# A shared expert's last result added in rows by fours, and expert weights asked for matrix by matrix

## The chip, the cores and the metric

One core of a Trainium2 chip runs the whole kernel. The metric is the device time of one execution in microseconds (us), the median of several runs. Engines are named as the profile names them: PE is TensorE's matmul, PEld its weight load, DVE is VectorE, ACT is ScalarE, POOL is GpSimd, SP is SyncE; a q behind a name is the engine's queue of instructions that issue DMAs or wait.

## The reference: what is computed

Inputs are x (4 sequences of 512 tokens, 512 features, float32) and a context (4 x 1601 x 512). The first half is a cross-attention with 16 heads over two groups of keys (1344 and 257), each with its own softmax, and a residual. The second half is a mixture of experts with a residual:

```
x  = x + cross_attention(layernorm(x), ctx)
h  = layernorm(x)                              # 2048 tokens x 512
idx, w = router(h)                             # 4 of 32 experts per token
for e in range(32):                            # at most 80 tokens each
    Y = (silu(X_e @ W_gate[e]) * (X_e @ W_up[e])) @ W_down[e]
    out[tokens of e] += Y * w
shared = (silu(h @ shared_gate.T) * (h @ shared_up.T)) @ shared_down.T
return x + out + shared
```

X_e are the tokens that chose expert e. W_gate[e] and W_up[e] are 512 x 256, W_down[e] is 256 x 512, all float32; the shared expert has 512 inner features.

## The kernel before, in words

A hand-written order of work (no scheduler) is recorded in Python, engine by engine. The attention of the four batches comes first. Then a stage of shared-expert units for batches 0 to 2 runs beside the routing, and from about 1477 us on the 32 experts follow one another.

**The shared expert.** `shared()` makes small units, each one matmul group of four matmuls: for each batch n, four `gate` and four `up` units that fill `hT` (512 inner features in four chunks of 128 partitions, by 512 tokens), then four `down` units, each with 128 tokens. For batches 0 to 2 (`n < BEFORE`, BEFORE is 3) `down` adds the residual row `x1r` and writes `out`. For the last batch, whose residual is already in `out`, `down` copies each 128 x 512 result into one chunk of the tile `ys` (L973), and the fourth one issues a single accumulating DMA from POOL that adds `ys` into the 512 rows of `out` (L976). In `ys` a partition p holds the tokens p, 128+p, 256+p and 384+p, so each of the 512 pieces is one row of 512 floats, 2 KB.

**The experts.** Turn e of the main loop records, in this order: `gate_up(e)` (32 matmuls of 80 columns), the gather of the tokens of e+7, `turn(e+2)` (transposes of gathered tokens), `down(e-1)` (two matmul groups of 512 columns, ACT's scaling into `y` at L1029, and POOL's indirect accumulating DMA that scatters the 80 rows of `y` into `out`, L1030), then the weights of expert e+4, and at certain turns one shared unit of the last batch, from the list `between` (12 units: eight gate and up, four down).

**What orders the DMAs.** Each scatter, and the shared accumulation, adds into `out`, so each waits on POOL's queue until the one ahead of it has landed. Gathers stand on the same queue between the scatters. Weights go over SP's queue, which holds nothing else in this stage. `expert_weights(e)` asks for `W_gate`, `W_up` and `W_down` of one expert (512 KB each, L908) into pools of five buffers each; a request waits on SP's queue until the matmuls that read its buffer are done. Called after `down(e-1)` for e+4, it takes the buffers of expert e-1. PSUM is a ring of eight banks.

The lines that place the shared units of the last batch (L1103):

```
while done < n_between and done * (E - 4) < n_between * (e + 1):
    between.pop(0)()
    done += 1
```

Of the kernel before, what the change touches and what calls it, by code (L numbers as in the profile page):

```python
# [9 lines left out]
F32 = mybir.dt.float32  # L10
BF16 = mybir.dt.bfloat16
I32 = mybir.dt.int32
AF = mybir.ActivationFunctionType
ALU = mybir.AluOpType
# [4 lines left out]
P = 128  # L19
B, L, D = 4, 512, 512  # L20
# [4 lines left out]
NC = D // P  # L25
NG4 = 4
NQ = L // P
T = B * L
NT = T // P
E, I, TOPK, NG, TKG = 32, 256, 4, 8, 3  # L30
EG = E // NG
CAP = 80
NI = I // P
# [25 lines left out]
@with_exitstack  # L59
def xattn_moe_kernel(ctx: ExitStack, tc: tile.TileContext, a: dict, out: bass.AP):  # L60
    nc = tc.nc

    dram = ctx.enter_context(tc.tile_pool(name="dram", bufs=1, space=DRAM))
    x1_d = dram.tile([T, D], F32, name="x1_d")

    xw_d = dram.tile([T, D + E], F32, name="xw_d")
    xnT_d = dram.tile([P, NC, T], F32, name="xnT_d")
    den_d = dram.tile([B * NC, 2 * NG4, L], F32, name="den_d")
    rec_d = dram.tile([B * NC, 2 * NG4, L], F32, name="rec_d")

    const = ctx.enter_context(tc.tile_pool(name="const", bufs=1))
    ident = const.tile([P, P], F32, name="ident")
    make_identity(nc, ident)
    mhalf = const.tile([P, 8], F32, name="mhalf")
    nc.gpsimd.memset(mhalf, -0.5)
    logits = const.tile([P, NT, E], F32, name="logits")

    with tc.manual_schedule():
        body(tc, a, ident, mhalf, logits, x1_d, xw_d, xnT_d, den_d, rec_d, out)


BEFORE = 3
# [27 lines left out]
def body(ctx, tc, a, ident, mhalf, logits, x1_d, xw_d, xnT_d, den_d, rec_d, out):  # L110

    nc = tc.nc
    early = ctx.enter_context(ExitStack())

    def pool(name, bufs, to=ctx, **kw):
        return to.enter_context(tc.tile_pool(name=name, bufs=bufs, **kw))
# [8 lines left out]
    def psum(dt=F32):  # L125

        shape = [P, 512] if dt is F32 else [P, NQ, P]
        banks.append(banks.pop(0))
        return ring.tile(shape, dt, name="ps", tag=f"bank{banks[-1]}")
# [8 lines left out]
    def wide(name, keep=False):  # L138

        n = wides.pop(0)  # L140
        t = pt.tile([P, NC, 512], F32, name=name, tag=f"wide{n}")
        if keep:
            return t, n
        wides.append(n)
        return t
# [4 lines left out]
    def held(name):  # L150
        return hold.tile([P, D], F32, name=name, tag="hold")
# [27 lines left out]
    _, n, s0, _ = BLOCKS[0]  # L179
# [42 lines left out]
    def project(ps, lhsT, rhs):  # L222

        for c in range(NC):
            nc.tensor.matmul(ps, lhsT=lhsT(c), rhs=rhs(c), start=c == 0, stop=c == NC - 1)
# [447 lines left out]
    for n in range(2):  # L673
        t = w.tile([P, NQ, P], BF16, name=f"parts{n}", tag=f"parts{n}")
# [6 lines left out]
    for b in range(B):  # L681
# [14 lines left out]
        ws = (wv, wvi)  # L696
# [73 lines left out]
        for bl in range(NB):  # L770
            for c in range(NC):
# [7 lines left out]
                n = 7 if bl < 2 else 0  # L779
# [16 lines left out]
        for c in range(NC):  # L796
# [7 lines left out]
            fill, done = [], 0  # L804
# [22 lines left out]
            for t in range(NKT):  # L827
# [8 lines left out]
                if t == 1:  # L836
                    if more:
# [3 lines left out]
                        done = 1  # L841
# [59 lines left out]
    aoT_last = aoT  # L901


    def expert_weights(e):
        ws = []
        for name, shape in (("W_gate", [P, NC, I]), ("W_up", [P, NC, I]), ("W_down", [P, NI, D])):
            t = wgp.tile(shape, F32, name=name, tag=name)
            nc.sync.dma_start(t, a[name][e])  # L908
            ws.append(t)
        return ws  # L910

    SHARE = 2.4
    AHEAD, WEIGHTS = 7, 5

    def tokens():

        past = ew.tile([E, CAP], F32, name="past", bufs=1)
        nc.vector.tensor_scalar(past, best, T + 0.5, float(T), ALU.is_gt, ALU.mult)
        nc.vector.scalar_tensor_tensor(past, past, float(T), best, ALU.add, ALU.subtract)
        ps = psum()  # L920
        nc.tensor.transpose(ps[:CAP, :E], past, ident[:E, :E])
        nc.vector.tensor_copy(tok, ps[:CAP, :E])

    def shared():


        units = [[], []]
        downs = []
        xTs = {0: first_xT[0]}

        def fetch_x(n):
            xTs[n] = wide("xT")
            nc.sync.dma_start(xTs[n], xnT_d[:, :, n * L:(n + 1) * L])

        for n in range(B):
            t = {}

            def gate(ic, n=n, t=t):
                if ic == 0:
                    t["hT"] = wide("hT")  # L940
                if ic == 2 and n + 1 < B:
                    fetch_x(n + 1)
                ps = psum()
                project(ps, lambda k: sg[:, k, ic * P:(ic + 1) * P], lambda k: xTs[n][:, k, :])
                nc.scalar.activation(t["hT"][:, ic, :], ps, AF.Silu)

            def up(ic, n=n, t=t):
                ps = psum()
                project(ps, lambda k: su[:, k, ic * P:(ic + 1) * P], lambda k: xTs[n][:, k, :])
                nc.vector.tensor_tensor(t["hT"][:, ic, :], t["hT"][:, ic, :], ps, ALU.mult)  # L950
                if n == 0 and ic == NC - 1:
                    wides.append(first_xT[1])

            def fetch(j, n=n, t=t):
                t[j] = held("x1r")
                nc.sync.dma_start(t[j], x1_d[n * L + j * P:n * L + (j + 1) * P, :])

            def down(j, n=n, t=t, fetch=fetch):
                rows = slice(n * L + j * P, n * L + (j + 1) * P)
                if n < BEFORE:  # L960
                    if j == 0:
                        fetch(0)
                    if j + 1 < NQ:
                        fetch(j + 1)
                ps = psum()
                project(ps, lambda k: t["hT"][:, k, j * P:(j + 1) * P], lambda k: sd[:, k, :])
                if n < BEFORE:
                    nc.vector.tensor_tensor(t[j], t[j], ps, ALU.add)
                    nc.sync.dma_start(out[rows, :], t[j])
                    return  # L970
                if j == 0:
                    t["ys"] = wide("ys")
                nc.scalar.copy(t["ys"][:, j, :], ps)  # L973
                if j == NQ - 1:
                    to = out[n * L:(n + 1) * L, :].rearrange("(j p) d -> p j d", p=P)
                    nc.gpsimd.dma_start(to, t["ys"], accum_op=ALU.add)  # L976

            to = units[n >= BEFORE]
            if n == BEFORE:
                units[0] += downs  # L980
                downs = []
            for ic in range(NC):
                to += [partial(gate, ic), partial(up, ic)]
                if ic < 2:
                    to += downs[2 * ic:2 * ic + 2]
            downs = [partial(down, j) for j in range(NQ)]
        units[1] += downs
        return units

    def expert_parts():  # L990
# [49 lines left out]
        return weights, gather, turn, gate_up, down  # L1040

    units, between = shared()
    wo = weight("o_w", wide("wo"))
    for u in units[:2]:
# [5 lines left out]
    wgp = pool("wgp", WEIGHTS, side="right", reuse_waits="tile")  # L1050
# [3 lines left out]
    weights, gather, turn, gate_up, down = expert_parts()  # L1054
# [9 lines left out]
    for i, u in enumerate(units):  # L1064
        if i < 2:
            continue
        if i == len(units) - 2:
            for f in first + second:
                f()
            first, second = [], []  # L1070
            tokens()
            for e in range(AHEAD):
                gather(e)
        u()
        for f in side.get(i, ()):
            f()
        later.step()
        if i == ready:

            space = mid.tile([P, 2, L], F32, name="rb")  # L1080
            second = sum(routing(B - 1, space.rearrange("p k t -> p (k t)")), [])

        while spent < (i - 1) * SHARE and (first or i > ready and second):
            todo = first or second
            spent += 0.8 if len(todo) < 2 * CAP // 8 else 0.3
            todo.pop(0)()
        if i % 4 == 0 and i // 4 - 1 < WEIGHTS:
            weights[i // 4 - 1] = expert_weights(i // 4 - 1)
    turn(0)
    turn(1)  # L1090
    n_between, done = len(between), 0
    for e in range(E + 1):
        if e < E:
            gate_up(e)
            if e + AHEAD < E:
                gather(e + AHEAD)
        if e + 2 < E:
            turn(e + 2)
        if e:
            down(e - 1)  # L1100
            if e + WEIGHTS - 1 < E:
                weights[e + WEIGHTS - 1] = expert_weights(e + WEIGHTS - 1)
        while done < n_between and done * (E - 4) < n_between * (e + 1):  # L1103
            between.pop(0)()
            done += 1

# [36 lines left out]
```

## Time and profile before

| what | value |
|---|---|
| median of 3 runs | 1721.97 us (1720.85 to 1722.82) |
| the profiled execution's own time | 1721.27 us |
| its span | 1719.6 us |
| granted TensorE clock, mean | 0.994 |
| PE busy | 1680.5 us (98%) |
| DVE, ACT, POOL busy | 981.4 us (57%), 651.1 us (38%), 864.5 us (50%) |
| W_gate, W_up, W_down requests | 32 of each, 512 KB a piece |
| the shared accumulation `out<-ys` | one, 1024 KB, issued at 1668.2 us |
| scatters `out<-y,tok` | 32, from 1493.2 to 1712.0 us |

The span is what the profile covers; the time of an execution is measured outside it and is 1.7 us longer here. A busy share is an average over stages: the attention, the shared units and routing, and the experts have different limits, and the last stage runs from about 1477 us to the end. In a timeline row the numbers are start, duration, engine, line, operation and tiles; the brackets hold the idle time before it and what ended that.

### The profile page before, as it was taken

What the parts mean: (1) busy time and instruction counts of PE and PEld (TensorE: products, weight loads), DVE (VectorE), ACT (ScalarE), POOL (GpSimd) and SP (SyncE); (2) the same over time, 40 slices, a digit from 0 to 9 for tenths busy, and PEclk for the clock granted to TensorE, in tenths of its full rate; (3) what the DMA queues carried; (4) which work ended last, traced back from release to release, by engine and by line L of the source; (5) the groups of instructions that cost most, each with busy time, mean ns of one, the idle gap of its engine ahead of it and who ended that gap; (6) DMA issues with size and microseconds to landing.
All of it is one profiled execution on the core that took longest, in us unless ns stands there. A gap on an engine that the chain in (4) does not pass through costs nothing. (4 is left out here: it accounts for less than half of the span.)

```text
span 1719.6 us, 29395 instructions
## 1 busy us (share of the span) xinstructions
PE 1680.5 (98%) x11753; PEld 880.9 (51%) x11753; DVE 981.4 (57%) x2016; ACT 651.1 (38%) x1378; POOL 864.5 (50%) x615
## 2 busy tenths in 40 slices
PE   8999999999999999999999999999999999999994
PEld 4564444456544444565444445644443454677773
DVE  3765554857555557976665579676657666111110
ACT  2135456611455565115555651145547210011111
POOL 3246977332668853327688533286792110333322
PEclk9999999999999999999999999999999999999997
DMA  7000000312000104020000040300012463588883
GB/s 231 1 1 1 27 27 2 122 56 80 20 2 26 27 10 156 21 80 13 19 10 27 14 151 21 105 14 14 2 30 94 147 238 101 183 268 272 274 252 56
DMA packets 68344, 137.34 MB, mean 80 GB/s; under 512 B 16112, under 2 KB 28528, under 8 KB 66160
## 3 DMA queue, kind: packets, MB, share of 16 engines
q1 hardware_dynamic: 61552, 122.01, 21.1%
q0 software_dynamic: 5648, 11.87, 3.4%
q8 instruction: 93, 1.52, 0.4%
q10 hardware_dynamic: 1008, 1.59, 0.3%
q14 instruction: 43, 0.35, 0.1%
HBM read 112.63 MB, written 22.81 MB: 79 GB/s over the span
## 5 line engine op out<-in xcount | busy, mean ns | idle before, releaser
L372 ACT ACTIVATE pT<-ps 128x512 f32<-128x512 f32 (+1 forms) x832 | 429.7, 603 | 342.2 <-PE ps L371 331.8
L334 DVE TENSOR_REDUCE mx<-ps 128x1 f32<-128x512 f32 (+1 forms) x576 | 330.8, 616 | 265.0 <-PE ps L320 265.0
L387 POOL TENSOR_TENSOR acc<-acc,pT 128x1024 f32<-128x1024 f32 x192 | 445.7, 2358 | 3.0 <-ACT pT L372 2.6
L379 PE MATMUL po<-pT,v 128*32 128x512 f32 (+2 forms) x1792 | 222.0, 603 | 0.0
L290 PEld LDWEIGHTS ps<-v_w,cT 128*128 128x128 f32 (+1 forms) x1408 | 168.9, 186 | 102.2 <-DVE mx L334 56.1
L371 PE MATMUL ps<-qT,kT 32*128 32x512 f32 (+1 forms) x1664 | 213.7, 587 | 0.0
L320 PE MATMUL ps<-kT,qT 32*128 32x512 f32 (+1 forms) x1536 | 206.1, 549 | 0.0
L290 PE MATMUL ps<-v_w,cT 128*128 128x128 f32 (+1 forms) x1408 | 197.7, 284 | 0.0
L231 PE MATMUL ps<-cT,wk 128*128 128x512 f32 (+1 forms) x384 | 155.9, 551 | 5.9 <-DMA wk<-in_k_w 5.9
L308 DVE TENSOR_REDUCE mx<-ps 128x1 f32<-128x512 f32 (+2 forms) x256 | 128.0, 561 | 5.2 <-PE ps L305 5.2
L1030 POOL DMA_INDIRECT out<-y,tok x32 | 45.5, 1423 | 151.6 <-DMA out<-y,tok 63.1
L231 PEld LDWEIGHTS ps<-cT,wk 128*128 128x128 f32 x384 | 70.3, 192 | 75.7 <-issue 55.1
L1020 DVE TENSOR_TENSOR ehT<-ehT,ps 128x160 f32<-128x160 f32 x32 | 10.3, 322 | 172.2 <-ACT ehT L1019 129.0
L368 PEld LDWEIGHTS <-pick 32*128 32x128 bf16 (+1 forms) x832 | 21.6, 91 | 165.8 <-issue 164.0
L298 ACT COPY v<-ps 128x128 f32<-128x128 f32 (+1 forms) x208 | 59.7, 287 | 117.8 <-PE ps L290 117.4
L238 POOL TENSOR_TENSOR sq_k<-sq_k,sq 128x512 f32<-128x512 f32 (+2 forms) x48 | 49.7, 1035 | 102.4 <-ACT sq L235 102.0
L394 POOL TENSOR_TENSOR acc<-pT 128x1024 f32<-128x1024 f32 x24 | 56.2, 2361 | 86.8 <-ACT pT L372 54.2
L387 POOL TENSOR_TENSOR pT<-pT 65x1024 f32<-65x1024 f32 x24 | 56.0, 2354 | 86.6 <-PE po L379 77.8
L387 DVE TENSOR_TENSOR acc<-acc,pT 128x1024 f32<-128x1024 f32 (+1 forms) x72 | 97.7, 1404 | 2.1 <-ACT pT L372 2.1
L320 PEld LDWEIGHTS ps<-kT,qT 32*128 32x128 f32 x1536 | 82.0, 183 | 30.8 <-issue 10.1
L379 PEld LDWEIGHTS po<-pT,v 128*32 128x32 f32 (+2 forms) x1792 | 34.7, 107 | 118.6 <-issue 109.3
L368 PE MATMUL ps<-mT,pick 32*128 32x512 bf16 (+1 forms) x832 | 82.5, 385 | 2.5 <-ACT mT L359 2.5
(209 smaller groups left out, 2188.5 us busy)
## 6 DMA issues: line engine op xcount, KB each, us to landing
W_gate<-in_W_gate SPq DMA_DIRECT2D x32, 512.0 KB
W_up<-in_W_up SPq DMA_DIRECT2D x32, 512.0 KB
W_down<-in_W_down SPq DMA_DIRECT2D x32, 512.0 KB
rb<-rec_d SPq DMA_DIRECT2D x64, 128.0 KB
xt<-in_x SPq DMA_DIRECT2D x30, 256.0 KB
cT<-in_ctxT SPq DMA_DIRECT2D x7, 1024.0 KB
wki<-in_k_img_w SPq DMA_DIRECT2D x4, 1024.0 KB
wo<-in_o_w SPq DMA_DIRECT2D x4, 1024.0 KB
```

The source lines that it names most:

```text
L231: nc.tensor.matmul(ps[:, :n], lhsT=wt[:, k, c * P:(c + 1) * P], rhs=xT[:, k, to], start=k == 0, stop=k == NC - 1)
L290: nc.tensor.matmul(ps[lo:hi, :], lhsT=cTs[bl][:, k, at:at + hi - lo], rhs=ws[bl == NB - 1][:, k, c * P:(c + 1) * P], start=k == 0, stop=k ...
L298: nc.scalar.copy(v[:n, t, :], ps[:n])
L308: nc.vector.tensor_reduce(mx[:, qt, g, bl:bl + 1], ps[:, :n], AX.X, ALU.max, negate=True)
L320: nc.tensor.matmul(ps[:, j * n:(j + 1) * n], lhsT=qT[r:r + HD, c, q * P:(q + 1) * P], rhs=kT[r:r + HD, c, k0:k0 + n], start=True, stop=True,)
L334: nc.vector.tensor_reduce(mx[:, qt, g, i:i + 1], ps[:, :m], AX.X, ALU.max, negate=True)
L368: nc.tensor.matmul(ps[:n], lhsT=pick[r:r + HD, kind(t), :n], rhs=mT[r:r + HD, :], start=True, stop=False)
L371: nc.tensor.matmul(ps[:n], lhsT=kT[r:r + HD, c, t * P:t * P + n], rhs=qT[r:r + HD, c, :], start=False, stop=True)
L372: nc.scalar.activation(pT[:n, g, :], ps[:n], AF.Exp)
L379: nc.tensor.matmul(po[r:r + HD, :], lhsT=v[rows, t, r:r + HD], rhs=pT[rows, g, :], start=start, stop=stop)
L387: (nc.vector if idle else nc.gpsimd).tensor_tensor(to[rows, h, :], to[rows, h, :], pT[rows, h, :], ALU.add)
L394: (nc.vector if idle else nc.gpsimd).tensor_tensor(acc[:, h, :], pTs[0][:, h, :], pTs[1][:, h, :], ALU.add)
```

## The change

Three edits. First, the last batch's tokens are laid out by fours: when `silu` and the multiply write `hT` for n = 3, they read the PSUM result with a step of four tokens, so chunk j of `hT` holds the tokens j, 4+j, 8+j and so on. Then partition p of `ys` holds the tokens 4p to 4p+3, which lie next to each other in `out`, and the accumulating DMA has 128 pieces of 8 KB (`"(p j) d -> p j d"` instead of `"(j p) d -> p j d"`). For n < 3 the new views name the same elements in the same order as before.

Second, `expert_weights` takes names: gate's and up's weights of expert e+5 are recorded right after `gate_up(e)`, down's of e+4 after `down(e-1)` as before. The first five experts' weights are asked for as before.

Third, each of the twelve shared units of the last batch is recorded one turn later. The accumulation then stands behind the scatter of expert 25 instead of that of expert 24.

```diff
-    def expert_weights(e):
-        ws = []
-        for name, shape in (("W_gate", [P, NC, I]), ("W_up", [P, NC, I]), ("W_down", [P, NI, D])):
-            t = wgp.tile(shape, F32, name=name, tag=name)
+    def expert_weights(e, *names):
+        for name in names or ("W_gate", "W_up", "W_down"):
+            t = wgp.tile([P, NI, D] if name == "W_down" else [P, NC, I], F32, name=name, tag=name)
             nc.sync.dma_start(t, a[name][e])
-            ws.append(t)
-        return ws
+            weights.setdefault(e, []).append(t)
...
+        def by_token(hT, ic):
+            return hT[:, ic, :].rearrange("p (j q) -> p j q", q=P)
+        def as_tiles(ps, n):
+            return ps.rearrange("p (j q) -> p j q", q=P) if n < BEFORE else ps.rearrange("p (q j) -> p j q", j=NQ)
...
-                nc.scalar.activation(t["hT"][:, ic, :], ps, AF.Silu)
+                nc.scalar.activation(by_token(t["hT"], ic), as_tiles(ps, n), AF.Silu)
...
-                nc.vector.tensor_tensor(t["hT"][:, ic, :], t["hT"][:, ic, :], ps, ALU.mult)
+                nc.vector.tensor_tensor(by_token(t["hT"], ic), by_token(t["hT"], ic), as_tiles(ps, n), ALU.mult)
...
-                    to = out[n * L:(n + 1) * L, :].rearrange("(j p) d -> p j d", p=P)
+                    to = out[n * L:(n + 1) * L, :].rearrange("(p j) d -> p j d", j=NQ)
                     nc.gpsimd.dma_start(to, t["ys"], accum_op=ALU.add)
...
             gate_up(e)
+            if e + WEIGHTS < E:
+                expert_weights(e + WEIGHTS, "W_gate", "W_up")
             if e + AHEAD < E:
                 gather(e + AHEAD)
...
             down(e - 1)
             if e + WEIGHTS - 1 < E:
-                weights[e + WEIGHTS - 1] = expert_weights(e + WEIGHTS - 1)
-        while done < n_between and done * (E - 4) < n_between * (e + 1):
+                expert_weights(e + WEIGHTS - 1, "W_down")
+        while done < n_between and done * (E - 4) < n_between * e:
```

More of the change, by code (lines that the diff above doesn't have):

```diff
@@ L1087, in body @@
         if i % 4 == 0 and i // 4 - 1 < WEIGHTS:
-            weights[i // 4 - 1] = expert_weights(i // 4 - 1)
+            expert_weights(i // 4 - 1)
     turn(0)
```

## The prediction

> **What bounds the kernel now.** I read the page's busy shares first, then the chain of waits that ended last, then the timeline of GpSimd, ScalarE, TensorE and SyncE over the last 60 us, and the DMA queues in the same stretch.
>
> ```profile
> span 1719.6 us, 29395 instructions
> PE 1680.5 (98%) x11753; PEld 880.9 (51%) x11753; DVE 981.4 (57%) x2016; ACT 651.1 (38%) x1378; POOL 864.5 (50%) x615
> DMA 1%; issue 0%; POOLq 0%
> DMA out<-y,tok 1%; POOLq L1139 0%; POOLq L1030 0%
> ```
>
> TensorE is busy for 98% of the span, but the chain that ended last consists of scatters (`out<-y,tok`). Both hold: TensorE sets the pace up to its last matmul, and a chain of accumulating DMAs sets the end. The timeline shows where one hands over to the other.
>
> ```profile
> 1659.30 0.68 ACT L1029 ACTIVATE y<-ps,xp 80x512 f32<-80x512 f32 x1 [1.74 <-PE ps L1025]
> 1668.26 0.68 ACT L1029 ACTIVATE y<-ps,xp 80x512 f32<-80x512 f32 x1 [1.74 <-PE ps L1025]
> ...
> 1697.32 0.68 ACT L1029 ACTIVATE y<-ps,xp 80x512 f32<-80x512 f32 x1 [1.29 <-DMA out<-y,tok]
> ```
> ```profile
> 1662.59 1.41 POOL L1030 DMA_INDIRECT out<-y,tok  x1 [6.44 <-DMA out<-y,tok]
> 1668.23 1.39 POOL L976 DMA_DIRECT2D out<-ys  x1 [4.22 <-DMA out<-y,tok]
> 1683.99 1.50 POOL L1030 DMA_INDIRECT out<-y,tok  x1 [14.37 <-DMA out<-ys]
> 1688.62 1.42 POOL L1030 DMA_INDIRECT out<-y,tok  x1 [3.12 <-DMA out<-y,tok]
> ...
> 1711.98 1.39 POOL L1030 DMA_INDIRECT out<-y,tok  x1 [3.31 <-DMA out<-y,tok]
> ```
>
> Columns: start, duration, engine, line, idle before and what ended it. I call the scatter of expert e s(e) and its input y(e). The three y rows are y(24), y(25), y(31); the GpSimd rows are s(24), the shared accumulation, s(25), s(26), s(31). Every accumulation waits for the one before it, because all add into `out`. The shared one holds the queue from 1668.23 to 1683.99, 15.76 us. y(25) is ready at 1668.94 and goes out 15 us late; from there seven scatters follow one another every 4.67 us ((1711.98-1683.99)/6), although y(31) is ready at 1698.0. So the end is s(31)'s issue plus 7.6 us, and whatever shortens the 15.76 us, or moves a scatter ahead of it, shortens the kernel, until y itself is late.
>
> Why 15.76 us? SyncE's rows and the queues in two stretches (1669 to 1674, 1674 to 1678) answer.
>
> ```profile
> 1668.21 0.33 SPq L908 DMA_DIRECT2D W_down<-in_W_down  x1
> 1668.58 0.43 SPq L908 DMA_DIRECT2D W_gate<-in_W_gate  x1
> 1669.06 0.43 SPq L908 DMA_DIRECT2D W_up<-in_W_up  x1
> 1673.74 0.33 SPq L908 DMA_DIRECT2D W_down<-in_W_down  x1
> ```
> ```profile
> q1 hardware_dynamic: 361, 1.35, 91.2%
> q0 software_dynamic: 17, 0.03, 4.2%
> ...
> q0 software_dynamic: 266, 0.54, 82.7%
> q1 hardware_dynamic: 89, 0.30, 23.8%
> ```
>
> Columns: packets, MB, share of 16 engines. The accumulation is issued together with 1.5 MB of weights, and while these pass (q1) it moves 17 of its 512 pieces. Its first packet starts 5.0 us after the issue, against 2.0 us for the undisturbed s(25). Then a 2 KB piece takes 0.199 us of a DMA engine (82.7% x 4 us x 16 / 266), which is 6.4 us for 512 pieces on 16 engines; the last W_down shares that stretch.
>
> **The change, part by part.** The twelve shared units move one expert later: unit k stood at the first e with 28k < 12(e+1), now at the first with 28k < 12e (old 0, 2, 4 ... 21, 23, 25; new 1, 3, 5 ... 22, 24, 26). TensorE has the same matmuls; a shared down unit takes 3.44 us (1659.05 to 1662.49). Around the end, y(23) and y(25) come 3.44 us earlier, y(24) and y(26) on stay; the accumulation stands behind s(25), with six scatters after it. TensorE waited for nothing in this stage, and the twelve moved units find their buffers as before: cost 0. Without a moved unit between them the first two experts run 5.53 us apart, as unseparated experts do later.
>
> Weights: gate's and up's requests of e+5 now follow gate_up(e), about 2.2 us (turn 0.27, down 1.71) before the end of down(e-1), behind which they stood on SyncE's queue; down's stays. The same 81 requests; nothing else is queued there in this stage. They were asked for four to five turns ahead, some 27 us, and TensorE never waited: gain 0, hidden by that distance; without it a 512 KB piece late by its own transit would cost about 1.5 us. What it does change is the collision: 1 MB now passes ahead of a scatter's issue, not with it.
>
> The permuted rows: for the last batch four silu (0.60 us each) and four multiplies (0.69 us) read PSUM with a step of four elements. No row shows such a read; bounds are 0 and four times, 1.8 to 2.1 us more each. ScalarE and VectorE are busy 7 and 5 of 40 us here, and the next instruction on either waits for a 3.5 us gate_up: hidden, 0. If it were not, each would hold a scatter by at most 2 us, and only the last of them would be near the end.
>
> The accumulation: 128 pieces of 8 KB instead of 512 of 2 KB. No row has an 8 KB accumulating piece. A plain 8 KB load takes 0.378 us of an engine (shared_up, 128 pieces, 37.8% x 8 us x 16), and a plain 2 KB one 0.082 (the context's rows of 512 tokens, 331 to 336: 85.6 us of engine time, less 67 pieces of 8 KB, over 736 of 2 KB), so accumulating adds 0.117 to a 2 KB piece. If that is per piece, eight pieces an engine take 8 x 0.495 = 4.0 us; if per byte, 6.4; plain loading alone would be 3.0, and 2 KB at the price of a lone scatter (0.257 each: 51.5% x 2.5 us x 16 / 80) 8.2. Both middle readings are equally near, so I take 5.2.
>
> **The sum.** s(24) goes out at y(24), 1659.98, plus 0.28: 1660.3. It lands in 5.6 (row 1662.59, weights running out) to 7.9 us (row before it, behind a full turn of weights); with 1 MB asked for at 1657.1 and 1662.6 I take 6.0, so s(25) goes at 1666.3. Weights ahead of it end by about 1667.6, so 5.64 again: the accumulation goes at 1671.9, well after the last ys copy (1668.2). Only the last W_down (1673.74) is beside it, 1.3 us of all engines. First packet 2.1 us after the issue, 1674.0; 5.2 + 1.3; 0.7 of late engines (1.4 in the row of before); 1.2 from the last packet to the next issue, as before: s(26) at 1682.4 instead of 1688.62. Five more steps of 4.67 and 7.6 us follow as now: 6.2 us less. The profiled execution (span 1719.6, time 1721.27) becomes 1715.1; it stands 0.7 under the median 1721.97, so I forecast 1715.8. TensorE's end, 1697, does not move.
>
> Bounds: s(25) at 1665.8 (y bound), landing in 4.65, 4.0 us and no late engines: s(26) at 1679.0, 9.6 us gained. s(24) with 7.9, s(25) 5.64, 8.2 us and 1.4: s(26) at 1688.0, 0.6 gained. y(29) (ready 1690.8), y(30) (1696.0) and y(31) limit the gain to about 10.7 (s(31) at 1701).
>
> **Rivals.** (1) An 8 KB piece costs no more than a plain load: 3.0 us, gain 8.4, 1713.6. For it: plain rates do not depend on the piece; against: accumulating doubled the 2 KB piece. The Trainium skill, "DMA: Bandwidth & Descriptors", "Anatomy of one DMA", gives 2.0 us plus bytes at 436 GB/s, an estimate of 4.4 us for this one and a gain at the limit, 10.7. By that a scatter's 164 KB would take 2.4 us; the trace has 4.65, so it does not hold for accumulations here.
>
> (2) The earlier gate and up requests land on s(24) and s(25) instead: both take 7.8 us, the accumulation goes at 1675.9 and costs by bytes (6.4, with 1.4 of late engines): s(26) at 1688.3, gain 0.3, 1721.7. For it: s(21) and s(23) took 7.6 and 7.9 behind weights. Against: those had 1.5 MB issued in the last 1.2 us before them, these 0.5.
>
> (3) Slower: an engine handles large read-and-add pieces one at a time, without the overlap that brought 0.257 down to 0.199. s(26) is 1677.2 plus eight pieces, so it decides from 1.43 us a piece, 1.8 times the price by bytes; at 2.06 (twice the lone price by bytes) 5.1 us more, 1727.1. Against: nothing in plain loads shows a penalty on size.
>
> (4) The pieces are cut back to 2 KB: 6.4 us, gain 5.0, 1717.0. In the built program the access on `out` is 128 rows of 2048 elements, which speaks against it. The Trainium skill, same page, "SDMA does more than copy", puts the limit of an accumulating element count at 2048, which these just meet; no run here shows it.
>
> **Chances.** Forecast (gain 4 to 8) 0.58, (1) 0.13, (2) with gains under 3.4 0.15, (3) 0.07, (4) 0.07. What a measurement of this kernel tells from no change is 0.2%, 3.4 us. Faster: 0.58 + 0.13 + 0.07 = 0.78; same: (2), 0.15; slower: (3), 0.07. The range takes the forecast, (1), (4) and the better part of (2): 1711.5 to 1720.0.
>
> **What would show it.** Right: the shared accumulation behind s(25), issued near 1672, with a first packet about 2 us later, 128 packets plus completions on q0, the next scatter 9 to 11 us after its issue, then six scatters 4.67 us apart, and y(31) unmoved. Wrong: a gap of over 16 us behind the accumulation (3), s(24) and s(25) at 7.8 us (2), or any TensorE wait for weights between 1480 and 1697, which would upset the sum altogether.

## The result and the profile after

The changed kernel takes 1718.42 us in the median (18 runs, 1713.75 to 1721.15) against 1721.96 before (18 runs, 1720.56 to 1722.99): a ratio of 0.9978, 95% interval 0.9972 to 0.9985, or 3.5 us less. The forecast was 6.2 us less: the sign was right, the size 2.7 us too large. The profiled execution took 1718.64 us with a span of 1716.8, so it is close to the median.

The page of the kernel after, first lines:

```profile
span 1716.8 us, 29451 instructions
PE 1681.6 (98%) x11753; PEld 881.2 (51%) x11753; DVE 981.4 (57%) x2016; ACT 650.6 (38%) x1378; POOL 864.1 (50%) x615
```

Engines do the same work as before. What changed stands in GpSimd's timeline (start, duration, engine, line, idle before it and what ended that): s(24), s(25), the shared accumulation, s(26) and s(31).

```profile
1663.80 1.41 POOL L1037 DMA_INDIRECT out<-y,tok  x1 [5.20 <-DMA out<-y,tok]
1670.73 1.39 POOL L1037 DMA_INDIRECT out<-y,tok  x1 [5.51 <-ACT ys L980]
1675.39 0.95 POOL L983 DMA_DIRECT2D out<-ys  x1 [3.27 <-issue]
1685.80 1.47 POOL L1037 DMA_INDIRECT out<-y,tok  x1 [9.45 <-DMA out<-ys]
...
1709.25 1.41 POOL L1037 DMA_INDIRECT out<-y,tok  x1 [3.32 <-DMA out<-y,tok]
```

The accumulation stands behind s(25) and holds the queue for 10.41 us instead of 15.76. s(26) goes out at 1685.80 instead of 1688.62, and s(31) 2.7 us earlier than before: the whole difference between the two profiled spans (2.8 us) is there before the tail begins. The tail itself still runs at 4.69 us a scatter.

SyncE's rows after show why the gap is shorter: gate's and up's last requests are out 11 to 13 us ahead of the accumulation, and only the last W_down (the second of the merged pair, 1675.4) meets it. The queues from 1678 to 1684 (packets, MB, share of 16 engines) show the accumulation nearly alone, in pieces of 8 KB: 1.03 MB in 132 packets.

```profile
1662.67 0.33 SPq L908 DMA_DIRECT2D W_gate<-in_W_gate  x1
1664.45 0.33 SPq L908 DMA_DIRECT2D W_up<-in_W_up  x1
1666.45 9.29 SPq L908 DMA_DIRECT2D W_down<-in_W_down  x2
```
```profile
q0 software_dynamic: 132, 1.03, 93.1%
q1 hardware_dynamic: 61, 0.18, 9.2%
```

The Trainium skill, "DMA: Bandwidth & Descriptors", "SDMA does more than copy", puts the largest element count of the accumulate (CCE) at 2048 on trn2. These rows agree as far as they go: pieces of 2048 float32 elements pass uncut, and no run here has larger ones.

### The profile page after: what moved, and what is told of

It reads as the page before. It is cut to its first block, busy times and chain, and to the rows that moved or that the text cites. A ratio compares the mean times of both kernels' runs of the same rounds, so it can differ in the third digit from the quotient of the medians.

```text
span 1716.8 us, 29451 instructions
## 1 busy us (share of the span) xinstructions
PE 1681.6 (98%) x11753; PEld 881.2 (51%) x11753; DVE 981.4 (57%) x2016; ACT 650.6 (38%) x1378; POOL 864.1 (50%) x615
```

## The experiments

All ratios are to the kernel before, run on the same chip in the same job; the changed kernel's is 0.9978 (0.9972 to 0.9985). The first kernels undo one edit or make one alone. A lag (the time from the moment a scatter's y is ready to the moment the scatter goes out) or a gap (the time that the accumulation holds the queue) is read from one profiled execution of each kernel. Those of weights undone, pieces undone, place undone, weights alone and place alone took 1.6 to 3.1 us longer than their kernel's median, so the median and the gap of these five need not belong together.

| kernel | 8 KB pieces | early gate and up | one turn later | ratio (95% interval) |
|---|---|---|---|---|
| changed | yes | yes | yes | 0.9978 (0.9972 to 0.9985) |
| weights undone | yes | no | yes | 0.9981 (0.9972 to 0.9990) |
| pieces undone | no | yes | yes | 0.9987 (0.9978 to 0.9996) |
| place undone | yes | yes | no | 0.9987 (0.9978 to 0.9996) |
| weights alone | no | yes | no | 0.9996 (0.9987 to 1.0006) |
| pieces alone | yes | no | no | 0.9978 (0.9968 to 0.9987) |
| place alone | no | no | yes | 0.9985 (0.9976 to 0.9994) |

**Weights undone.**

```diff
-            if e + WEIGHTS < E:
-                expert_weights(e + WEIGHTS, "W_gate", "W_up")
...
-                expert_weights(e + WEIGHTS - 1, "W_down")
+                expert_weights(e + WEIGHTS - 1)
```

> The changed kernel with the weight requests as before (all three of e+4 after down(e-1)); the 8 KB pieces and the later place stay. Theory A: the spread requests of gate and up keep every scatter behind weights, so the chain of scatters lags and the shared accumulation goes out 3.5 us later than forecast (1675.4 instead of 1671.9). Undone, scatters alternate again between one that goes out at its y and one that waits, the accumulation goes out near 1672 and the time is about 1715, 3.5 us under the changed kernel. Theory B: a scatter beside weights takes about 7.2 us in whatever order they are asked for, and the lag comes from the new places of the shared units: 1718.4, no difference from the changed kernel, accumulation near 1675.

Measured: 1717.62 us, ratio 0.9981. Neither forecast holds whole. s(24) goes out at its y, as theory A said (lag 0.28 us against 2.14 in the changed kernel), but s(24) and s(25) take 7.5 and 6.4 us, so the accumulation still goes out at 1675.2. One W_down passes beside it as in the changed kernel (144 packets in both), and it holds the queue for 11.10 us instead of 10.41. The time is nearer to theory B.

**Pieces undone.**

```diff
-            return ps.rearrange("p (j q) -> p j q", q=P) if n < BEFORE else ps.rearrange("p (q j) -> p j q", j=NQ)
+            return ps.rearrange("p (j q) -> p j q", q=P)
...
-                    to = out[n * L:(n + 1) * L, :].rearrange("(p j) d -> p j d", j=NQ)
+                    to = out[n * L:(n + 1) * L, :].rearrange("(j p) d -> p j d", p=P)
```

> The changed kernel with the shared accumulation in 512 pieces of 2 KB (tokens in the old order, no stepped reads); weights and place as changed. Both theories: the accumulation goes out where the changed kernel's does; 0.199 us for a 2 KB piece against the 0.71 us that the 8 KB piece takes in the trace after make 6.4 against 5.7 us of transfer, so 0.7 us slower, 1719.1. If making 512 descriptors delays the first packet as well, the gap behind the accumulation grows from 10.4 to 13 us and the time is near 1721.

Measured: 1718.56 us, ratio 0.9987. The time is near the first theory, but neither had the rest: the accumulation goes out at 1677.67, 2.3 us later than in the changed kernel, when the last weights have 0.34 MB left, which passes ahead of its first packet. It holds the queue for 9.91 us, no longer than with 8 KB pieces. In this place the pieces buy nothing that these runs can tell: the two intervals overlap.

**Place undone.**

```diff
-        while done < n_between and done * (E - 4) < n_between * e:
+        while done < n_between and done * (E - 4) < n_between * (e + 1):
```

> The changed kernel with the shared units at their old turns, so that the accumulation stands behind the scatter of expert 24; weights and 8 KB pieces as changed. Theory A: the early requests still make scatters lag, the accumulation goes out near 1669 to 1671, still meets the last 1 to 1.5 MB of weights and holds the queue for 12 to 13 us: 1719 to 1720.5. Theory B: the lag belongs to the new places, so it is gone; accumulation at 1668, 12 us: 1717.5 to 1718.5.

Measured: 1718.38 us, ratio 0.9987; the accumulation goes out at 1670.78 and holds the queue for 11.46 us. Again between the theories: it starts late as A said, the gap is shorter than either said, and the time is B's.

**Weights alone** (the kernel before with the early requests).

```diff
+            if e + WEIGHTS < E:
+                expert_weights(e + WEIGHTS, "W_gate", "W_up")
...
-                weights[e + WEIGHTS - 1] = expert_weights(e + WEIGHTS - 1)
+                expert_weights(e + WEIGHTS - 1, "W_down")
```

> The kernel before with the early requests of gate and up alone. Theory A: every scatter a little later, the accumulation goes out 1 to 3 us later than at 1668.2, but meets less weight traffic: 1721 to 1724, no better than before. Theory B: the requests do nothing, 1722 within 1 us.

Measured: 1720.60 us, ratio 0.9996: no difference that can be told. The trace shows two things that cancel: the scatters lag more (5.55 us at s(24) against 2.61 before), so the accumulation goes out at 1673.79 instead of 1668.23; but by then most weights have passed, and it takes 11.63 us instead of 15.76. In the profiles of the four kernels with early requests the mean lag of s(3) to s(24) behind their y is 2.2, 2.7, 2.8 and 4.1 us; in the four without, 1.6, 1.7, 1.8 and 2.1. Across the four pairs that differ in this edit alone the ratio moves by -0.0004, +0.0009, +0.0002 and -0.0003: the lag is longer with the early requests, but no help or harm to the time can be told.

**Pieces alone** (the kernel before with the 8 KB pieces and the stepped reads that go with them).

```diff
-                    to = out[n * L:(n + 1) * L, :].rearrange("(j p) d -> p j d", p=P)
+                    to = out[n * L:(n + 1) * L, :].rearrange("(p j) d -> p j d", j=NQ)
```

> The kernel before with the 8 KB pieces alone. Trace after: an 8 KB piece takes 0.71 us of a DMA engine, four times the 0.18 of an unobstructed 2 KB one, so the price goes by bytes. Theory P (by bytes, the pieces do nothing): the accumulation still goes out with 1.5 MB of weights at 1668 and holds the queue for 15 to 16 us, 1721.5 within 0.7. Theory Q (fewer pieces get through the weights better, because each turn of the queue carries four times the bytes): the gap shrinks to 12 to 13 us and the time is 1718.5 to 1719.5.

Measured: 1717.25 us, ratio 0.9978: theory Q. That the time lies 1.3 us under its range is mostly the job: the kernel before took 1720.99 us in this one and 1721.96 in that of the result. This edit alone gives as much as all three. The accumulation goes out where it did before, together with the same 1.5 MB of weights, and holds the queue for 12.18 us. GpSimd's rows, then the queues from 1673 to 1678:

```profile
1668.73 0.95 POOL L983 DMA_DIRECT2D out<-ys  x1 [4.53 <-DMA out<-y,tok]
1680.91 1.47 POOL L1037 DMA_INDIRECT out<-y,tok  x1 [11.23 <-ACT y L1036]
```
```profile
q0 software_dynamic: 101, 0.83, 81.3%
q1 hardware_dynamic: 98, 0.40, 21.2%
```

101 pieces of the accumulation pass beside 98 of the weights, one for one, and since its pieces are twice as large as a weight's (8 against 4 KB) it gets two thirds of the bytes. Done after 128 pieces, it leaves weights to go last: some 140 of their 516 packets in this gap follow its last one, while in the kernel before all 576 pass before the accumulation is through. They do no harm there, because TensorE needs them much later.

That is only about half of what the gap lost. From first to last packet the accumulation takes 7.9 us here against 9.5 before, but its first packet also comes 3.2 us after the issue instead of 5.1, behind 107 weight packets instead of 325. The sharing of the queues doesn't explain this second part. The weights were asked for 0.2 us later against its issue than before, and whether the larger pieces have a part in it isn't shown.

**Place alone** (the kernel before with the units one turn later).

```diff
-        while done < n_between and done * (E - 4) < n_between * (e + 1):
+        while done < n_between and done * (E - 4) < n_between * e:
```

> The kernel before with the shared units one turn later, alone. Theory P: this is the edit that pays; the accumulation, 2 KB pieces, goes out near 1675 with one W_down beside it and holds the queue for 10 to 11 us, 1717.6 as with the 8 KB pieces (the run with the weights undone), within 0.8. Theory Q: without the large pieces the gap stays at 13 us or more, 1720 to 1721.

Measured: 1717.96 us, ratio 0.9985; accumulation at 1674.94, 11.85 us. The time agrees with theory P to 0.4 us, the ratio with that of the run which theory P names (0.9981) to 0.0004; the gap is 0.9 us above it. Only 144 weight packets pass beside the accumulation, against 576 before. So two edits each lessen the same collision, and together they can't lessen it twice: that fits 0.9981 for both of them without the weights' edit, where the product of 0.9978 and 0.9985 would be 0.9963.

**No weights after the first five experts.** The next two kernels request no further weights, so expert e computes with those of e-5; the second has 2 KB pieces, by the edit of "Pieces undone".

```diff
-            if e + WEIGHTS < E:
-                expert_weights(e + WEIGHTS, "W_gate", "W_up")
...
-                expert_weights(e + WEIGHTS - 1, "W_down")
+                weights[e + WEIGHTS - 1] = weights[e - 1]
```

> The changed kernel without any weight request after the first five experts: expert e uses the weights of e-5, so the output is another. It measures what weights cost the chain. If the scatters' 7 us are weights: every scatter takes 4.7 to 5 us and goes out at its y, the accumulation goes out near 1673 and holds the queue for 9 to 10 us (2.0 to the first packet, 5.7, late engines and completion 1.9); 1713 to 1715. If scatters are slow for another reason (their own rows, gathers beside them), they stay at 7 us and the time at 1718.

> The run without later weights, with 512 pieces of 2 KB. Theory P: the accumulation holds the queue as long as with 8 KB pieces, within 0.7 us. If fewer, larger pieces are cheaper by themselves: 2 KB takes 1.5 us more or worse.

Measured: 1713.77 us with 8 KB pieces, 1713.32 with 2 KB, one run each. GpSimd's rows of the accumulation and s(26), first 8 KB, then 2 KB:

```profile
1671.61 0.95 POOL L983 DMA_DIRECT2D out<-ys  x1 [3.13 <-issue]
1681.44 1.47 POOL L1037 DMA_INDIRECT out<-y,tok  x1 [8.89 <-ACT y L1036]
```
```profile
1671.37 1.39 POOL L983 DMA_DIRECT2D out<-ys  x1 [3.04 <-issue]
1680.93 1.51 POOL L1037 DMA_INDIRECT out<-y,tok  x1 [8.17 <-DMA out<-ys]
```

9.83 us and 9.56: without company the larger pieces gain nothing, and 1 MB takes about 7.2 and 6.5 us from first to last packet. And every scatter from s(0) to s(25) goes out 0.28 us behind its y, even where two y are only 5.5 us apart, so each takes less than that. What GpSimd waited for from 1480 to 1660 without weights, then in the kernel after from 1480 to 1670 (total us, times, longest):

```profile
POOL out L1037 <- ACT y L1036: 107.9, 24, 7.5
```
```profile
POOL out L1037 <- DMA out<-y,tok: 74.2, 16, 5.6
POOL out L1037 <- ACT y L1036: 31.5, 7, 6.2
```

Without weights it waits for y alone; with them mostly for the scatter ahead. So the scatters' 7 us are weights. What weights still cost the changed kernel is some 3.5 us, an estimate from the ratios (1713.77 / 1720.99 = 0.9958, one run, against 0.9978).

**Weights in 2 KB pieces** (the kernel before, each weight asked for as two halves).

```diff
-            nc.sync.dma_start(t, a[name][e])
+            for h in range(2):
+                part = slice(h * shape[1] // 2, (h + 1) * shape[1] // 2)
+                nc.sync.dma_start(t[:, part, :], a[name][e][:, part, :])
```

> The kernel before with each expert weight asked for as two halves, so that weights too pass in 2 KB pieces (256 KB a request). Theory R (a DMA engine takes turns between the two queues, one piece each): beside 2 KB weights the 2 KB accumulation gets twice the share it had beside 4 KB ones, and the gap behind it shrinks from 15.8 to 12.5 to 14 us: 1718.5 to 1720.5. Rival S (the weights that were asked for first simply go first, whatever the pieces): gap 15 to 16 us, 1721 to 1722.5.

Measured: 1721.87 us, ratio 1.0002 (0.9993 to 1.0012). The gap is 14.68 us, 1.1 less than before and more than theory R said. The queues from 1674 to 1681:

```profile
q0 software_dynamic: 451, 0.92, 72.2%
q1 hardware_dynamic: 431, 0.80, 35.6%
```

The equal turns are there, 451 pieces to 431, but the forecast of theory R fell, in gap and time. The first 3.2 us behind the issue still belong to the weights ahead, and then nearly all that is left of them passes before 512 pieces are through: 10.4 us from first to last packet against 9.5 before. The gap is shorter only by its earlier start. The time is that of rival S, the gap is just under its range.

**All three weights together.**

```diff
                 expert_weights(e + WEIGHTS, "W_gate", "W_up")
+            if WEIGHTS <= e + WEIGHTS - 2 < E:
+                expert_weights(e + WEIGHTS - 2, "W_down")
...
-            if e + WEIGHTS - 1 < E:
-                expert_weights(e + WEIGHTS - 1, "W_down")
```

> The changed kernel with down's weights of e+3 asked for together with gate's and up's of e+5, right after gate_up(e), so that all three are asked for some 3 us before the next scatter goes out instead of up to its very issue. If a scatter's 7 us come from weights asked for in the 2 us before it: scatters land in 5 to 6 us, the lag at s(24) is 0.3, the accumulation goes out near 1672 and holds the queue for 10 us: 1714.5 to 1716. If only the amount of weight traffic counts: lag and time as in the changed kernel, 1717.5 to 1718.5.

Measured: 1721.52 us, ratio 0.9997 (0.9988 to 1.0006). The idea fell: scatters that waited for the one ahead took 7.2 us each as elsewhere, the mean lag rose to 4.7 us, and the gain of the changed kernel is gone. Its profiled execution (1718.50) is the fastest of its 11, so its trace does not show the usual case, and where the median loses 3 us stays open.

**Four additions.** On top of that:

```diff
-            return ps.rearrange("p (j q) -> p j q", q=P) if n < BEFORE else ps.rearrange("p (q j) -> p j q", j=NQ)
+            return ps.rearrange("p (j q) -> p j q", q=P)
...
-                if j == NQ - 1:
-                    to = out[n * L:(n + 1) * L, :].rearrange("(p j) d -> p j d", j=NQ)
-                    nc.gpsimd.dma_start(to, t["ys"], accum_op=ALU.add)
+                nc.gpsimd.dma_start(out[rows, :], t["ys"][:, j, :], accum_op=ALU.add)
```

> The run with the weights together, and the shared result of each 128 tokens added by a DMA of its own (256 KB, 2 KB pieces, tokens in the old order) right after its unit, so that three of the four additions fall into the 9 us between two experts that a shared unit separates. If scatters land in 5 us there is room for a 5 us addition in those gaps and only the last one counts: 1712 to 1714. If scatters keep taking 7 us, four additions of 5 to 7 us take the place of one of 10: 1722 to 1730.

Measured: 1732.03 us, ratio 1.0061 (1.0047 to 1.0074), slower as its second case said, and 2 us beyond that range. Two rows of GpSimd's timeline, an addition of 256 KB and the scatter behind it:

```profile
1633.48 0.96 POOL L981 DMA_DIRECT2D out<-ys  x1 [7.67 <-ACT y L1034]
1642.26 1.47 POOL L1035 DMA_INDIRECT out<-y,tok  x1 [6.51 <-ACT ys L980]
```

8.8 us for a quarter of the bytes; the other three additions took 8.1, 4.8 and 4.7 us. A chain with no slack can't be lengthened: the scatters fall 24 us behind, the four y buffers fill, and y(31) is ready only at 1709.4, 11 us later than before.

**Two turns later** (8 KB pieces, weights as before).

```diff
-        while done < n_between and done * (E - 4) < n_between * (e + 1):
+        while done < n_between and done * (E - 4) < n_between * (e - 1):
```

> The kernel before with the 8 KB pieces and the shared units two turns later instead of one, so that the accumulation stands behind the scatter of expert 26, when the last weights have gone. If all that is left to gain is the collision with weights: the accumulation goes out near 1680 and holds the queue for 9.8 us as without weights, the scatter of expert 27 goes out near 1689.8 as with the pieces alone: 1717 to 1717.5, no better than the pieces alone. If the gap behind the accumulation sets the time by itself, 2 us less than with the pieces alone: 1715 to 1715.5.

Measured: 1716.54 us (7 runs, 1715.66 to 1716.81), ratio 0.9971 (0.9960 to 0.9982), the lowest of the kernels that ask for all weights, and in between the two cases. GpSimd's rows:

```profile
1679.50 0.95 POOL L983 DMA_DIRECT2D out<-ys  x1 [3.14 <-DMA out<-y,tok]
1688.14 1.47 POOL L1037 DMA_INDIRECT out<-y,tok  x1 [7.70 <-DMA out<-ys]
```

8.64 us, without weights beside it, and s(27) at 1688.14 against 1690.47 in the changed kernel. It beats the kernel before; its interval overlaps the changed kernel's, so that it beats that one too isn't shown.

## Why the prediction was right or wrong

**The bound.** Right: the end hangs on the chain of additions into `out`, and s(31) and the end moved together. y(31) did not stay where it was, as forecast: it was ready at 1699.42, 1.4 us later. s(31) still went out 9.8 us behind it, so y did not set the end.

**The gap.** Forecast 10.5 us (1671.9 to 1682.4), measured 10.41. Its parts were off and cancelled, so the agreement is luck. The piece price that I put halfway (0.65 us) was 0.71 us in the mean of the 128 pieces, which is 5.7 us for eight on an engine where I had 5.2. By bytes it is no cheaper than 2 KB, as the two runs without weights show. The last W_down and the late engines (the DMA engines that finish last) were 2.0 us in the sum; together they added some 0.7 us, for a total of 6.3 from first to last packet, because 107 of the 144 weight packets passed ahead of the first piece. And that first packet came after 2.9 us, not 2.1.

**The start of the gap: the term that was mis-sized.** The accumulation was to go out at 1671.9 and went out at 1675.39, 3.5 us later, which is all that the forecast of s(26) lacked (1682.4 against 1685.80). By the steps of the sum: y(24) was ready 1.7 us later than in the profile before, of which 1.07 is there already at the first gate_up (1480.19 against 1479.12; the profiles of all kernels lie between 1479.1 and 1480.6) and 0.6 is lost behind it: from there to y(24) it takes 181.5 us against 180.9. In that stretch TensorE stands idle for 0.28 us in the middle of the second expert's gate matmuls (1485.33), released by nothing that the profile shows. Five of the eight profiles with units one turn later have such a stop and take 181.3 to 181.5 us; place alone and the two without weights have none and take 180.9, as the old places do. Its cause is open. Then s(24) went out 2.14 us behind y(24), not 0.28; it took 6.93 us, not 6.0; s(25) took 4.66, not 5.64. Together 1.68 + 1.86 + 0.93 - 0.98 = 3.49. The failing sentence is "s(24) goes out at y(24)": I had read the scatters of the kernel before as bound by y and hurt by weights now and then, while 13 of its 23 from s(0) to s(22) made the next one wait, at 7.25 us each, against one y every 7.0 us in the mean ((1659.98 - 1492.92) / 24, from y(0) to y(24)). So the chain has no slack to make up a delay, and its lag moves with the traffic: at s(24) it was between 0.28 and 5.55 us in the profiles of the kernel before and the seven of the table. Rival (2) had nearly the right place for the accumulation (1675.9), but by another path: it let s(24) and s(25) take 7.8 us each, and they took 6.93 and 4.66; and its gap, 12.4 us, was 2 us too long.

**What the edits were worth.** I priced the place as the main gain and the pieces as 1.2 us (rival (4) against the forecast). In the old place the pieces alone give it all, and not by a cheaper byte. The sum had no term for the cause: more bytes in each turn beside the weights are about half of the shorter gap, an earlier first packet of unknown cause is the other half. The place alone gives 0.9985. Rival (1) fell, since 2 KB and 8 KB take the same time undisturbed; (3) and (4) did not happen.

**Hidden edits.** Right: the stepped reads cost nothing (silu 597 ns for all 16, multiply 657 to 689), the profile shows no wait of TensorE for a weight, and the weights' edit is worth nothing that can be told, though its lag and its shorter gap cancel rather than both being 0.

## What to carry to other kernels

Where several DMAs add into one tensor, look for the chain of them beside the busiest engine, and compare the time of one link under load with the interval at which links arrive: when they are equal, there is no slack to move work into. A large transfer that must get through another queue's traffic can be helped by larger pieces even if its price by bytes stays, and by a place where that traffic has ended; both remove the same collision, so test them one at a time before adding them up.

## What the runs showed of the hardware

While both queues have work, the DMA engines serve them at equal numbers of pieces: 101 to 98 with 8 and 4 KB, 451 to 431 with 2 and 2 KB. The Trainium skill, "DMA: Bandwidth & Descriptors", "Queues, rings and completion order", says that an engine goes round its queues packet by packet, with typically 9 to 17 descriptors in a packet. The equal counts agree with equal turns; being sums over 16 engines, they don't show how many pieces go in one turn.

What differs is the start. Where weights were asked for within a microsecond of the accumulation's issue, its first piece came 2.4 to 5.1 us after the issue (weights undone, kernel before), and only weights moved until then. Without weights it came after 1.5 to 2.0 us, and after 1.6 and 2.0 where the weights ahead had been asked for at least 1.5 us earlier (place undone, pieces undone). Why is open.

The changed kernel's runs spread over 7.4 us, those of the kernel before over 2.4. A lag that differs from run to run would do that; no two profiles of the same kernel were compared, so it isn't shown.
